# The second graph layer of a graph and expert kernel: 512 of 3125 destinations aggregated by row fetches instead of matrix products

## The chip, the cores and the metric

The kernel runs on one core of one Trainium2 chip. The time is the device time of one execution in microseconds (us). Times of single instructions come from one profiled execution. The engines are TensorE (PE; PEld is its weight load), VectorE (DVE), ScalarE (ACT), GpSimd (POOL) and SyncE (SP, which here only issues DMAs).

## The reference

A graph of 3125 nodes with 256 features and 103125 edges (sorted by destination, each node with a loop to itself) goes through four blocks, each added to its input: three graph attention layers, 16 experts of which each node uses two, one graph sum layer, and 8 experts of which each node uses one. The change concerns the second attention layer:

```python
def _gat_layer(x, src, dst, W, al, ar, b, n_nodes):
    h = x @ W
    el = h @ al
    er = h @ ar
    e = jax.nn.leaky_relu(el[src] + er[dst], NEG_SLOPE)
    m = jax.ops.segment_max(e, dst, num_segments=n_nodes)
    ex = jnp.exp(e - m[dst])
    s = jax.ops.segment_sum(ex, dst, num_segments=n_nodes)
    alpha = ex / s[dst]
    out = jax.ops.segment_sum(alpha[:, None] * h[src], dst, num_segments=n_nodes)
    return out + b
```

A destination has 33 edges on average.

## The kernel before, in words

Nodes lie in NT = 25 tiles of 128. `dense_attention` first builds a matrix of edge counts (uint8, sources on partitions, destinations along the row) and uses it in all three attention layers. The counts come from `Locator`, which reads the sorted edge lists with indirect DMAs (`find`, L1590) and sorts them into windows of five destinations (`finish`), and from `Counter`, which makes one-hot tiles on VectorE and ScalarE (L1662 to L1668), multiplies them on TensorE (L1683) and writes the counts with ScalarE (L1693). All this happens during the first layer.

The exponential of a leaky ReLU of el + er is factored: exp(0.2 el) is multiplied into the source row, and what is left per edge is max(exp(0.8 el), exp(-0.8 er)), up to a factor that cancels in the division. `Sources` holds this for one layer: `h` (25 tiles of 257 columns, the last one the factor itself, so that its sum is the divisor), `rho` = exp(0.8 el) and `lr`, the two products. `put` makes a tile of it: products (L1142), `lr` on VectorE (L1145), two exponentials and a scaled copy on ScalarE (L1146 to L1149).

A layer runs over 13 groups of destinations (`GROUPS`: 12 of 256, one of 53) and in each over the 25 source tiles s. One step is: VectorE makes a mask `pm` of 128 x 256 out of the destination terms `tau`, `rho` and the counts (L1310), and TensorE multiplies its two halves with the source row tile into two accumulators (L1313, in float32, two records per product). `pm` has six buffers. The last, small group makes six masks at a time (`few`, L1302, L1304) and uses half tiles (L1306). `terms` (L1250, L1253) makes `tau` for the next group at step 18, but for a layer's first group only when the layer begins. After a group, `divide` (at step 8 of the next group; L1339, L1340, L1348) divides by the sum and adds the bias, and `onward` (steps 10 and 13, one for each of the two tiles) transposes on TensorE (L1361), applies the ReLU on ScalarE (L1363) and calls `put` for the next layer's sources. In the third layer the result goes to a router instead.

While the first layer runs, `spare_rows` has GpSimd clear two tiles (L1320) and SP write them to the experts' row tables in DRAM in 34 transfers (L1727, up to 2.5 MB each). The order of instructions on each engine is set by a planner that uses its own estimates of durations and the order of issue; no order is written by hand.

Of the kernel before, what the change touches and what calls it, by code (L numbers as in the profile page):

```python
# [1 line left out]

# [7 lines left out]
F32 = mybir.dt.float32  # L10
# [712 lines left out]
def routed_experts(tc, x, room, ident, rows, sums, places, w1, w2, w3, load):  # L723
# [10 lines left out]
    with tc.tile_pool(name="rw", bufs=3) as ep, tc.tile_pool(name="rx", bufs=2) as xp, \  # L734
# [99 lines left out]
        def turn_more(slot, xs, s, own):  # L834
            ps = tp.tile([P, nh, P], F32, name="ps_x")
            for j in range(nh):
                nc.tensor.transpose(ps[:, j], s[:, j * P:(j + 1) * P], ident)
            hid = mp.tile([P, nh, P], F32, name="hid1")
            nc.scalar.copy(hid, ps)
            return slot, xs, hid, own  # L840
# [235 lines left out]
FINISH = [(0, 20), (2, 16), (4, 4), (5, 16)]  # L1076
TERMS = 18
EARLY = 8
SOME = 6
HELD = 64.0  # L1080

# [34 lines left out]
def block(big, d=D):  # L1116

    return big.tile([P, NT * (D + 1)], F32, name="big")[:, :NT * d].rearrange("p (t d) -> p t d", d=d)


class Sources:
# [3 lines left out]
    def __init__(self, tc, big, small):  # L1125
        self.nc = tc.nc
        self.h = block(big, D + 1)
        self.rho = small.tile([P, NT], F32, name="rho")
        self.lr = small.tile([P, 2, NT], F32, name="lr")

        for to in (self.h[:, NT - 1], self.rho[:, NT - 1:], self.lr[:, :, NT - 1]):
            self.nc.gpsimd.memset(to, 0.0)

    def put(self, pp, t, r, xTs, w, at=()):


        nc, n = self.nc, len(xTs)
        pss = []
        for i, xT in enumerate(xTs):
            ps = at[i] if i < len(at) else pp.tile([P, D + 2], F32, name="ps_m")  # L1140
            for k in range(KD):
                nc.tensor.matmul(ps[:r], xT[:, k], w[:, k], start=(k == 0), stop=(k == KD - 1))  # L1142
            pss.append(ps)
        for i, ps in enumerate(pss):
            nc.vector.tensor_scalar(self.lr[:r, :, t + i], ps[:r, D:], -HELD, HELD, op0=OP.max, op1=OP.min)  # L1145
        nc.scalar.activation(self.h[:r, t:t + n, D], self.lr[:r, 0, t:t + n], AF.Exp, scale=0.2)  # L1146
        nc.scalar.activation(self.rho[:r, t:t + n], self.lr[:r, 0, t:t + n], AF.Exp, scale=0.8)
        for i, ps in enumerate(pss):
            nc.scalar.activation(self.h[:r, t + i, :D], ps[:r, :D], AF.Copy, scale=self.h[:r, t + i, D:])  # L1149


def dense_attention(tc, dram, counts, x_in, big, ident, eps, layers, src, dst, rows, high, make_router, over):

# [9 lines left out]
    with tc.tile_pool(name="dw", bufs=1) as cp, tc.tile_pool(name="dwl", bufs=2) as wl, \  # L1163
         tc.tile_pool(name="dsm", bufs=2) as small:
        top = cp.tile([P, 3], F32, name="top")
        x = block(big)
        with tc.tile_pool(name="dp", bufs=6) as pmp, tc.tile_pool(name="ds", bufs=2) as sp, \
# [10 lines left out]
            kp = first.enter_context(tc.tile_pool(name="dpc", bufs=2, space=PSUM))  # L1178
            counter = Counter(tc, lp, ohp, locator, counts)
            pairs = [range(-(-c // (BATCH * WIN)), -(-(c + n) // (BATCH * WIN))) for c, n in GROUPS]  # L1180

# [63 lines left out]
            def terms(now, a):  # L1245
# [8 lines left out]
                return tau  # L1254

            third = ExitStack()
            later = []
            fills = []
            for i in range(3):
                last = i == 2  # L1260
                bt_i = bt
                if last:
                    wp = third.enter_context(tc.tile_pool(name="ro", bufs=2))
                    rp = third.enter_context(tc.tile_pool(name="ror", bufs=4))
                    zp = third.enter_context(tc.tile_pool(name="rop", bufs=1, space=PSUM))
                    router = make_router(third.enter_context(tc.tile_pool(name="roc", bufs=1)))
                    y_out = block(big)
                    nc.gpsimd.memset(y_out[:, NT - 1], 0.0)
                    nxt, we_n = None, None
                else:  # L1270
                    nxt = Sources(tc, big, small)
                    we_n, bt, products = attention_weights(tc, wl, cp, layers, i + 1, now.rho[:, NT - 1:])
                    products()
                for a, (c, n) in enumerate(GROUPS):
                    tiles = [(q, (c + q) // P, min(P, n - q)) for q in range(0, n, P)]

                    edges = counts_of(counts, a)
                    ahead = list(pairs[a + 1]) if i == 0 and a + 1 < len(GROUPS) else []
                    ready = []
                    tau = tau_next if a else terms(now, 0)  # L1280
                    acc = ap_.tile([P, 2, CHUNK], F32, name="acc")
# [7 lines left out]
                    for s in range(NT):  # L1289
                        if s == TERMS and a + 1 < len(GROUPS):  # L1290
                            tau_next = terms(now, a + 1)
                        if i == 0 and (a, s) in FINISH:
                            locator.finish(FINISH.index((a, s)) + 1, pp)
                        if i == 0 and (a, s) in FIND:
                            locator.find(FIND.index((a, s)) + 1, kp, tau[:, 0:1])
                        while later and later[0][0] == s:
                            later.pop(0)[1]()
                        if n <= P // 2:
                            if s % SOME == 0:
# [5 lines left out]
                            at = s % 2 * (P // 2)  # L1305
                            nc.tensor.matmul(acc[at:at + n, 0, :D + 1], few[:, s % SOME], now.h[:, s], start=(s < 2),  # L1306
                                             stop=(s >= NT - 2))
                        else:
                            pm = pmp.tile([P, PAIR], F32, name="pm")
                            nc.vector.scalar_tensor_tensor(pm[:, :n], tau[:, :n], now.rho[:, s:s + 1],  # L1310
                                                           edges[:, s, :n], op0=OP.max, op1=OP.mult)
                            for j, (q, t, r) in enumerate(tiles):
                                nc.tensor.matmul(acc[:r, j, :D + 1], pm[:, q:q + r], now.h[:, s], start=(s == 0),  # L1313
                                                 stop=(s == NT - 1))
                        while ready and ready[0][0] <= s:
                            counter.add(kp, ready.pop(0)[1])
                        if s == 2 and fills:

                            for e in empties:
                                nc.gpsimd.tensor_scalar(e, tau[:, 0:1], 0.0, None, op0=OP.mult)  # L1320
# [30 lines left out]

                    sooner = 2 if a == len(GROUPS) - 2 else 0
                    later.append((8 - sooner, divide))
# [3 lines left out]
                    for j, (q, t, r) in enumerate(tiles if not last else []):  # L1357
                        def onward(j=j, t=t, r=r, rest=rest, nxt=nxt, w=we_n):
                            ps = pp.tile([P, KD, P], F32, name="ps_m")
# [4 lines left out]
                            nxt.put(pp, t, r, [yT[:, :, :r]], w)  # L1364
                        later.append((10 + 3 * j, onward))
                    if i == 0 and a == 1:
                        fills, empties = spare_rows(tc, cp, *rows)
                if i == 0:
                    first.close()
                nc.vector.tensor_reduce(top[:, i:i + 1], now.lr, AX.XY, OP.max, apply_absolute_value=True)  # L1370
                now = nxt
            for _, what in later:
                what()
            router.finish(wp, zp, over)
            ps = pp.tile([3, P], F32, name="ps_m")
            nc.tensor.transpose(ps, top, ident)
            most = cp.tile([3, 1], F32, name="most")
            nc.vector.tensor_reduce(most, ps, AX.X, OP.max)
            ps = pp.tile([1, 3], F32, name="ps_m")
            nc.tensor.transpose(ps, most, ident[:3, :3])  # L1380
            nc.vector.tensor_reduce(high, ps, AX.X, OP.max)
# [137 lines left out]
class Locator:  # L1519
# [8 lines left out]
    def __init__(self, tc, cp, dram, src, dst, ident, room):  # L1528
# [36 lines left out]
        def find(j, pp, behind=None):  # L1565
# [8 lines left out]
            for q in range(NHEAD):  # L1574
                nc.tensor.matmul(ps[:PW], less[:rows, q, :PW], one[:rows], start=(q == 0), stop=(q == NHEAD - 1))
            at = cp.tile([P, 1], I32, name=f"at{j}")
            nc.vector.tensor_scalar(at[:PW], ps[:PW], -1.0, 0.0, op0=OP.add, op1=OP.max)
            if j < PARTS - 1:
                nc.vector.tensor_scalar(at[:PW], at[:PW], float(NR - RE // ER), None, op0=OP.min)
            for u, (of, name) in enumerate(self.lists):  # L1580
                if j == PARTS - 1:

                    to = dram.tile([E + RE], I32, name=name)
                    nc.sync.dma_start(to[:E].rearrange("(p e) -> p e", p=rows), of.rearrange("(p e) -> p e", p=rows))
                    none = cp.tile([1, RE], I32, name=name)
                    nc.gpsimd.memset(none, -WIN)
                    nc.sync.dma_start(to[None, E:], none)
                    of = to
                of = of.rearrange("(t e) -> t e", e=ER)
# [116 lines left out]


def spare_rows(tc, cp, rows0, rows1):

# [21 lines left out]
def routed(ctx: ExitStack, tc: tile.TileContext, i: dict, out: bass.AP, over):  # L1731
# [12 lines left out]
    with tc.tile_pool(name="counts", bufs=1) as kp:  # L1744
        counts = kp.tile([P, NT * ((len(GROUPS) - 1) * PAIR + 64)], U8, name="counts")
        x = dense_attention(tc, dram, counts, i["x"], big, ident, eps, layers, i["src"], i["dst"], (rows0, rows),
                            over[:, 3:4], lambda cp: Router(tc, cp, ident, eps, iota, count, rows0, sums,
                                                            i["L0_ffn_gate_w"], i["L0_ffn_gate_b"], more), over[:, 0:1])
        with tc.tile_pool(name="s0", bufs=1) as sp:
# [101 lines left out]
```

## Time and profile before

| | us |
|---|---|
| three runs, median (lowest to highest) | 1865.95 (1864.18 to 1867.11) |
| the profiled execution | 1866.04 |
| its span, first to last instruction | 1864.3 |
| first layer's steps begin | 72.0 |
| second layer's steps begin | 456.3 |
| third layer's steps begin | 755.5 |
| third layer ends, about | 1047 |

In the profile a group of instructions has its line in the kernel, engine and operation, then output <- inputs, shapes and a count, then busy time and the mean time of one in ns, and at last the idle time of that engine just before them with what ended it. In an order of time a line has start, length, engine, line, operation, names and how many instructions were merged into it. Matrix products overlap, so a single product's 382 ns is more than its share of the time: four of them follow each other in 0.87 us.

### The profile page before, as it was taken

Reading aid. Unit: us, or ns where it says so; the run is one execution under the profiler, and the core shown is the slowest. Engines: PE = TensorE matmul, PEld = TensorE weight load, DVE = VectorE, ACT = ScalarE, POOL = GpSimd, SP = SyncE. Lnnn points to the kernel's source line nnn. Section 1 sums busy time; section 2 is a strip of 40 time slices with the busy share of each in tenths; the row PEclk is TensorE's granted clock in tenths of the full one; section 3 lists DMA queues with packets and bytes.
Section 4 is the critical chain, followed back from the end, with each engine's and each line's share of the span. In section 5 each row is a group of like instructions: output and inputs, shape, how many; then the busy total and the mean of one; then the engine's idle time right before and its main releaser. Section 6 shows DMA issues by size and latency. Waiting matters only on the chain. (4 is left out here: it accounts for less than half of the span.)

```text
span 1864.3 us, 27270 instructions
## 1 busy us (share of the span) xinstructions
PE 1808.2 (97%) x9423; PEld 1427.1 (77%) x9423; DVE 971.2 (52%) x2644; ACT 717.5 (38%) x2052; POOL 309.6 (17%) x461
## 2 busy tenths in 40 slices
PE   6999999999999999999999799999989999999997
PEld 4788888887888888788888566666768886555886
DVE  5888888875555555677777622222252222224221
ACT  3766677671011111122222221211138998444221
POOL 4210100000000000133332322333300000222222
PEclk9999999999999999999999899999999999999999
DMA  3111113757000000111111286767430001733664
GB/s 116 33 36 46 48 62 129 312 213 306 1 1 1 1 1 7 41 46 46 46 46 42 76 261 188 213 180 200 91 80 1 1 1 35 245 128 143 219 211 129
DMA packets 105783, 185.42 MB, mean 99 GB/s; under 512 B 10968, under 2 KB 73849, under 8 KB 105600
## 3 DMA queue, kind: packets, MB, share of 16 engines
q1 hardware_dynamic: 74060, 127.06, 20.2%
q0 software_dynamic: 16432, 34.02, 6.9%
q10 hardware_dynamic: 15138, 22.44, 3.7%
q8 instruction: 79, 1.29, 0.3%
q14 instruction: 74, 0.61, 0.1%
HBM read 95.80 MB, written 89.77 MB: 100 GB/s over the span
## 5 line engine op out<-in xcount | busy, mean ns | idle before, releaser
L1313 PE MATMUL acc<-big,pm 128*128 128x257 f32 x3600 | 828.1, 382 | 3.1 <-DVE pm L1310 3.1
L1313 PEld LDWEIGHTS acc<-big,pm 128*128 128x128 f32 x3600 | 667.6, 190 | 94.6 <-DVE pm L1310 4.8
L1310 DVE SCALAR_TENSOR_TENSOR pm<-tau,rho,counts 128x256 f32<-128x256 f32 x900 | 427.5, 487 | 211.1 <-PE acc L1313 203.5
L774 PE MATMUL ps_h<-xsT,w 128*128 128x384 f32 x512 | 168.4, 487 | 0.6 <-ACT xsT L750 0.6
L1440 PE MATMUL acc<-msg,cr 128*128 128x512 f32 (+1 forms) x625 | 157.7, 403 | 0.1
L774 PEld LDWEIGHTS ps_h<-xsT,w 128*128 128x128 f32 x512 | 96.8, 190 | 66.9 <-issue 1.9
L1440 PEld LDWEIGHTS acc<-msg,cr 128*128 128x128 f32 (+1 forms) x625 | 114.7, 185 | 29.1 <-ACT cr L1436 1.2
L1436 ACT ACTIVATE cr<-counts 128x256 fp32r<-128x256 uint8 (+1 forms) x325 | 130.5, 402 | 14.4 <-PE acc L1440 6.9
L1693 ACT CAST counts<-acc_c 128x500 uint8<-128x500 f32 (+1 forms) x155 | 96.0, 678 | 93.9 <-PE acc_c L1683 93.8
L1023 PE MATMUL ps_y<-t_wd,hsT 128*128 x480 | 108.8, 380 | 0.4 <-ACT hsT L1051 0.4
L1668 DVE TENSOR_TENSOR ohk<-iota_k,key 128x2016 f16<-128x2016 f16 (+1 forms) x79 | 94.4, 1195 | 22.2 <-PE acc_c L1683 22.2
L777 ACT ACTIVATE silu<-ps_h 128x384 f32<-128x384 f32 x64 | 31.4, 491 | 182.1 <-PE ps_h L774 182.1
L1363 ACT ACTIVATE yT<-ps_m 128x256 f32<-128x256 f32 (+1 forms) x50 | 18.7, 375 | 214.4 <-PE ps_m L1361 214.4
L1023 PEld LDWEIGHTS ps_y<-t_wd,hsT 128*128 128x128 f32 x480 | 88.8, 190 | 11.6 <-ACT hsT L1051 0.6
L778 DVE TENSOR_TENSOR hid<-silu,ps_h 128x384 f32<-128x384 f32 x64 | 35.5, 554 | 114.4 <-PE ps_h L774 108.9
L1662 ACT ACTIVATE ohs<-iota_s,low 128x128 f16<-128x128 f16 x286 | 94.1, 401 | 0.0
L929 PE MATMUL ps_H<-big,t_w 128*128 128x512 f32 (+1 forms) x224 | 93.1, 552 | 0.7 <-ACT H L931 0.5
L794 POOL DMA_INDIRECT sums<-y,who x48 | 74.9, 1560 | 94.0 <-DVE y L792 70.3
L789 PE MATMUL ps_o<-w,hid 128*128 128x256 f32 x384 | 87.2, 379 | 0.0
L1683 PEld LDWEIGHTS <-ohs 128*128 128x128 f16 x1250 | 77.7, 98 | 10.9
L1683 PE MATMUL acc_c<-ohk,ohs 128*128 128x125 f16 x1250 | 84.5, 218 | 0.0
L789 PEld LDWEIGHTS ps_o<-w,hid 128*128 128x128 f32 x384 | 71.0, 190 | 8.8
(324 smaller groups left out, 1938.9 us busy)
## 6 DMA issues: line engine op xcount, KB each, us to landing
rows<-empty SPq DMA_DIRECT2D x16, 2564.0 KB, 18.6
w<-in_L_ffn_w_dram ACTq DMA_DIRECT2D x42, 512.0 KB, 4.9
hs<-rows SPq DMA_DIRECT2D x29, 641.0 KB, 4.3
big<-in_L_ffn_w_dram SPq DMA_DIRECT2D x30, 512.0 KB, 6.1
rows<-empty SPq DMA_DIRECT2D x16, 516.0 KB, 5.0
t_wd<-in_L_ffn_Wd_dram SPq DMA_DIRECT2D x8, 1024.0 KB, 11.9
xs<-rows SPq DMA_DIRECT2D x15, 387.0 KB, 3.4
bias<-in_L_ffn_bd_dram SPq DMA_DIRECT2D x30, 128.0 KB, 4.0
```

Source lines behind the costliest of these rows:

```text
L774: nc.tensor.matmul(ps, w[:, k, j * P:(j + 1) * P], xsT[:, k], start=(k == 0), stop=(k == KD - 1))
L789: nc.tensor.matmul(ps, hid[:, j, q * P:(q + 1) * P], o[:, j], start=(j == 0), stop=(j == nh - 1))
L929: nc.tensor.matmul(ps[:, :n], a[:, k, j * P:(j + 1) * P], xnT[:, k, c:c + n], start=(k == 0), stop=(k == KD - 1))
L1023: nc.tensor.matmul(ps, hsT[:, j], d[:, ds(e, 1), j, :].rearrange("p o f -> p (o f)"), start=(j == 0), stop=(j == nh - 1))
L1310: nc.vector.scalar_tensor_tensor(pm[:, :n], tau[:, :n], now.rho[:, s:s + 1], edges[:, s, :n], op0=OP.max, op1=OP.mult)
L1313: nc.tensor.matmul(acc[:r, j, :D + 1], pm[:, q:q + r], now.h[:, s], start=(s == 0), stop=(s == NT - 1))
L1436: nc.scalar.activation(cr[:, :n], edges[:, s, :n], AF.Copy, accum_out=seen[:, a * NT + s:a * NT + s + 1])
L1440: nc.tensor.matmul(acc[:r, j].rearrange("p h d -> p (h d)"), cr[:, q:q + r], msg[:, s].rearrange("p h d -> p (h d)"), start=(s == 0), stop ...
L1662: nc.scalar.activation(far[:, i], self.iota_s, AF.Abs, scale=-1.0, bias=self.low32[:, batch, i:i + 1])
L1668: nc.vector.tensor_tensor(to[:, i:tiles].rearrange("p t (x u) -> p t x u", u=2), iota.rearrange("p (x u) -> p x u", u=2)[:, None].to_broad ...
L1683: nc.tensor.matmul(acc[:, u], ohs[:, i], ohk[:, i, :KEYS], start=(t == 0), stop=(t == TW - 1))
L1693: nc.scalar.copy(to[:, :, d0 % PAIR:d0 % PAIR + whole * WIN].rearrange("p s (u d) -> p u s d", u=whole), acc[:, :whole])
```

## The change

In the second layer (i == 1) the loop over groups leaves out the first two (`APART` = 2, so `FEW` = 4 tiles, 512 destinations). For these a new class `Apart` follows the edges themselves:

- Each source tile of the second layer has `rho` in the same row as `h` (258 columns), and each tile, when made, is also written to a table in DRAM (`save`, 25 transfers by SP).
- During the first layer `bounds` and `rank` find, for each of the 512 destinations, where its edges begin and how many it has, and gather the edges' source numbers (`who`, five indirect DMAs). A destination has 38 places (`OWN`); what is over goes to a fifth tile of at most 128 destinations with 20 more places (`HEAVY`). These are 4 x 38 + 20 = 172 columns.
- In the second layer GpSimd fetches for each column one row per destination from the table (172 indirect DMAs of 128 rows of 258 words), in 45 batches of up to four, five batches ahead (`RING`). VectorE makes the coefficients of a batch and adds coefficient times row to an accumulator, one instruction per column. The fifth tile's sums are spread back to their destinations by one product on TensorE for each of the four tiles (`expand`).
- These pieces are placed between the steps of the remaining groups by a formula: column q at 19 + 1.31 q us, with 0.976 us per step. In this layer each engine keeps the order of issue (`manual_schedule`), and the way onward is cut in three pieces at steps +0, +1 and +4 with a copy of the raw product in between.
- The terms of the next layer's first group are made in the group before. The third layer's first group takes the source tiles from the fifth on, the first four last.
- One tile in the last expert block (`hid`) is now an earlier tile reused.

The core of the diff:

```diff
 class Sources:
-        self.h = block(big, D + 1)
-        self.rho = small.tile([P, NT], F32, name="rho")
+        self.h = block(big, ROW)
+        self.rho = self.h[:, :, D + 1]
...
+            def onward_steps(at, y, t, r, name, nxt, w, save):
...
+                return [(at, turn), (at + 1, multiply), (at + 4, keep)]
...
+                order = ExitStack()
+                if apart_now:
+                    order.enter_context(tc.manual_schedule())
                 for a, (c, n) in enumerate(GROUPS):
+                    if apart_now and a < APART:
+                        continue
...
-                    tau = tau_next if a else terms(now, 0)
+                    tau = tau_next or terms(now, a)
...
-                        if s == TERMS and a + 1 < len(GROUPS):
-                            tau_next = terms(now, a + 1)
+                        now_step[0] = (a - APART) * NT + s
+                        if s == (EARLIER if apart_now else TERMS):
+                            if a + 1 < len(GROUPS):
+                                tau_next = terms(now, a + 1)
+                            else:
+                                tau_next = None if last else terms(nxt, 0 if apart_now else APART)
...
+                            of = (s + FEW) % NT if last and a == 0 else s
...
+                        if apart_now and (a, s) == (APART, BEGIN):
+                            apart.begin(hp, hq, pp, now.lr)
+                        if apart_now and (a, s) == (APART, FETCH):
+                            for b in range(RING):
+                                apart.fetch(b)
+                        while soon and soon[0][0] <= now_step[0]:
+                            soon.pop(0)[1]()
+                        while now_apart and now_apart[0][0] <= now_step[0]:
+                            now_apart.pop(0)[1]()
...
+class Apart:
...
+    def save(self, sources, t, r):
+        self.nc.sync.dma_start(self.table[t * P:t * P + r], sources.h[:r, t])
...
+    def begin(self, hp, hq, pp, lr):
...
+        self.hots(hot)
...
+        for t in range(FEW):
+            nc.tensor.transpose(ps[:, t], hot[:, t], self.ident)
+        nc.scalar.copy(self.back, ps)
+        self.tau = hp.tile([P, FEW + 1], F32, name="apart_tau")
+        nc.scalar.activation(self.tau[:, :FEW], lr[:, 1, :FEW], AF.Exp, scale=-0.8)
+        ps = pp.tile([P, 1], F32, name="ps_m")
+        for t in range(FEW):
+            nc.tensor.matmul(ps, hot[:, t], self.tau[:, t:t + 1], start=(t == 0), stop=(t == FEW - 1))
+        nc.scalar.copy(self.tau[:, FEW:], ps)
...
+    def fetch(self, b):
...
+        for j in range(BATCHES_OF[b][2]):
+            nc.gpsimd.indirect_dma_start(
+                out=row[:, j], out_offset=None, in_=self.table[:, :],
+                in_offset=bass.IndirectOffsetOnAxis(ap=self.who[:, q + j:q + j + 1], axis=0))
...
+        def at(q):
+            time, whole = LANDED + EVERY * q, STEP * NT * (len(GROUPS) - 1 - APART)
+            return math.ceil(time / STEP if time < whole else whole / STEP + (time - whole) / LAST_STEP)
...
+            nc.vector.scalar_tensor_tensor(co[:, :m], row[:, :m, D + 1], self.tau[:, t:t + 1], self.real[:, q:q + m],
+                                           op0=OP.max, op1=OP.mult)
...
+                nc.vector.scalar_tensor_tensor(state["acc"], row[:, j, :D + 1], co[:, j:j + 1], state["acc"],
+                                               op0=OP.mult, op1=OP.add)
...
+            nc.tensor.matmul(ps, self.back[:, t], state["heavy"], start=True, stop=True)
```

## The prediction

> **What bounds the kernel now.** I read the summary of engines first, then the second graph layer alone as a stretch, TensorE's order of time through one of its groups, and last the rows of GpSimd and VectorE that can price the new work.
>
> ```profile
> PE 1808.2 (97%) x9423; PEld 1427.1 (77%) x9423; DVE 971.2 (52%) x2644; ACT 717.5 (38%) x2052; POOL 309.6 (17%) x461
> ```
>
> TensorE is busy for 97% of the span. The stretch of the second layer (first to last aggregation; columns: stretch, length, then PE, PEld, DVE, ACT, POOL busy, clock, DMA share, GB/s) says it more sharply:
>
> ```profile
> 456.30:755.50 299.20, 298.14 (x1426) 255.68 (x1426) 165.33 (x390) 32.42 (x115) 2.40 (x6) 1.00 0.01 4
> ```
>
> PE is busy 298.1 of 299.2 us, VectorE 165, GpSimd 2.4, the DMA engines 1%. So TensorE's work is this layer's length, and the units that the change loads are nearly idle. In order of time on PE, one group:
>
> ```profile
> 512.75 0.38 PE L1361 MATMUL ps_m<-ident,y 128*128 128x128 f32 x2
> 512.97 1.03 PE L1313 MATMUL acc<-big,pm 128*128 128x257 f32 x4
> 513.84 1.03 PE L1142 MATMUL ps_m<-we,yT 128*128 128x258 f32 x4
> ...
> 521.88 0.38 PE L1250 MATMUL ps_m<-ident,lr 128*128 128x128 f32 x2
> 522.09 14.92 PE L1313 MATMUL acc<-big,pm 128*128 128x257 f32 x68
> 536.85 0.38 PE L1361 MATMUL ps_m<-ident,y 128*128 128x128 f32 x2
> ...
> 755.47 8.95 PE L1313 MATMUL acc<-big,pm 128*128 128x257 f32 x40 [1.06 <-DVE pm L1310]
> ```
>
> A group of 256 destinations repeats every 536.85 - 512.75 = 24.10 us. One step (four records of L1313) takes 513.84 - 512.97 = 0.87 us, and 25 of them 21.7; the rest is two passes onward per group (transpose 0.22, product 0.87: 1.09 us each) and the 0.21 of the destination terms. The last line is the next layer's start: PE waits 1.06 us there for the first mask.
>
> The rows that price the change, first VectorE, then GpSimd:
>
> ```profile
> 455.75 3.26 DVE L1310 SCALAR_TENSOR_TENSOR pm<-tau,rho,counts 128x256 f32<-128x256 f32 x8 [1.69 <-ACT tau L1253]
> 447.96 0.49 DVE L1304 TENSOR_TENSOR few<-few,counts 128x318 f32<-128x318 f32 x1
> ```
> ```profile
> 125.28 1.28 POOL L1590 DMA_INDIRECT counts<-in_src_dram,at x1 [0.30 <-issue]
> ```
> ```profile
> L676 POOL DMA_INDIRECT rows<-row,g_to x50 | 50.5, 1009 | 41.1 <-DVE pm L1310 23.7 <-issue 10.7 <-DVE g_to L669 3.0
> L978 POOL DMA_INDIRECT rows<-row,to x25 | 24.5, 980 | 94.0 <-ACT row L974 72.0 <-ACT H L931 13.4 <-issue 4.3
> ```
>
> Eight masks run in 3.26 us: 0.41 us each when nothing holds them. An indirect DMA costs GpSimd 0.98 to 1.01 us as a scatter and 1.28 as a gather, and 0.30 us before the next one.
>
> [...] L676, issued in the third layer beside the masks, ranges from 0.972 to 1.085 us, L978 mostly stays at 0.975. [...] L676 lands 2.6 us after issue, the gathers of L1590 4.5.
>
> **The change part by part.** The layer's 12 full groups become 10. In program order of the changed kernel I count 50 masks and 100 aggregation products fewer, 172 row fetches on GpSimd, 172 sums and 45 coefficient operations on VectorE.
>
> *Removed on PE.* Two groups, 2 x 24.10 = 48.2 us.
>
> *Kept or added on PE.* Their four tiles still go onward: 4 x 1.09 = 4.4. Four spreading products of 257 columns, two records each: 4 x 0.43 = 1.7. At the first step four transposes and four one-column products, in order on PE: they wait for VectorE's four one-hot tiles, then for ScalarE's copy and exponential. Transposes 0.9, the copy of 512 columns about 0.6 (the same-sized copy hsT<-ps_cols has 0.589), exponential 0.2, products about 0.9, waits about 0.5: 3.1 us.
>
> *Starts of layers.* The terms of the next layer's first group are now made before it begins; the 1.06 us idle goes at both starts.
>
> *First layer.* Finding each destination's edges adds some 10 small products (1.2 us of PE), about 25 VectorE operations (some 10 us beside 305 busy in 375), five gathers and 25 saves of 128x258 rows. VectorE has slack and masks may run six steps ahead (six buffers, 5.2 us), which hides bursts of 3 to 4 us; I allow 1 us. Without that cover: 10 us. The saves share SP's queue with the 2.5 MB fills (L1727); only the last one matters, since the first fetch waits for it. In the trace the DMAs of the fills are done about 5 us into the layer, GpSimd's last clear at 461.4; the last save is issued at step 9 (9 x 0.964 + 3.1 = 12 us in) and lands in about 2.4 (row y<-in_x, same size), so the first fetch starts about 15 us into the layer. The first sum stands at step 25, about 27 us. Four fetches and a landing, 15 + 4 x 1.31 + 4.5 = 25, arrive before it.
>
> *GpSimd's fetches.* The code sets one sum per 1.31 us of an assumed step of 0.976; at the real 24.10/25 = 0.964 that is 1.294 us per sum. Fetches take duration + 0.30. Bounds: 0.975 + 0.30 = 1.28 (scatter) and 1.33 + 0.30 = 1.63 (median of the gathers of L1590). I take 1.31, as L676: it has the same 128 rows of 258 words and runs beside masks, whereas L1590 takes 125 rows and runs beside the f16 compares. Then GpSimd is busy 172 x 1.31 = 225 of 260 us and a deficit of 172 x 0.016 = 2.7 us meets a lead of about 2. Each fetch is refilled some 20 sums ahead, so landing is hidden. A fetch moves 132 KB; L676's DMAs, the same size, ran at this rhythm.
>
> *VectorE.* Per sum of 1.294 us: masks 1.34 x 0.41 = 0.55; the sum 0.41 to 0.53 (L1304, which needs the result before it, starts 0.53 after that), middle 0.45; coefficient 0.05; the rest, of the divisions and small columns, 0.08. Together 1.13, 87%: close, but below PE. VectorE runs in order, so a late row holds the masks queued behind that sum, and PE waits for these.
>
> *ScalarE* gains a 0.4 us copy per tile (the raw products), in a layer where it is 11% busy: nothing. Order of issue replaces a planner's order; in both, the product stands one step (0.87 us) behind its transpose, and the ReLU between takes 0.38. I allow 2 us for collisions with the passes of the four tiles and late rows.
>
> *Other edits.* The strides of 258, the in-place hid and the rotated sources of the third layer's first group: no time by themselves; the rotation lets the four tiles come last.
>
> **Sum.** Second layer after: 10 x 24.10 = 241.0, the small group 755.47 - 745.05 - 1.06 = 9.4, onward 4.4, spreading 1.7, first step 3.1, collisions 2.0: 261.6, against 755.47 - 456.29 = 299.2: minus 37.6. First layer: + 1.2 + 1.0 - 1.06 = + 1.1. Together - 36.5. The profiled execution took 1866.04 (span 1864.3 and 1.7 around it), 0.1 above the median 1865.95 of the runs; so 1866.0 - 36.5 = 1829.5.
>
> **Rivals.** *Rows later than planned, part of the gain lost (1838 to 1862).* If a fetch costs 1.45 us [...], the last row lands at 15 + 172 x 1.45 + 3 = 267.4, and the 9 us of the small group come after it: 276.8, 15 more, 1845. A sum that costs 0.7 instead of 0.45 makes VectorE the bound at about 1.38 per sum and gives 172 x 0.09 = 15 too. For it: the 0.972 to 1.085 spread. Against: the spread is a tenth only, with VectorE 75% busy there (194 of 260 us, 770 to 1030).
>
> *Slower: the gather's own price.* If direction, not the 125 rows or the f16 compares, makes L1590 dear, then 1.63 holds: 15 + 172 x 1.63 + 4.5 + 9.4 = 309, 10 more than now; with the first layer's 1.1, 1877. It is slower from about 1.57 us per fetch. For it: the only gathers in the trace cost that, to 1.28 at the least. Against: L676's rows are those of the fetches, L1590's 125 partitions are not. That VectorE is 87 to 89% busy beside L1590 (stretches 72 to 130 and 130 to 200) cuts both ways: it may be why they are slow, and VectorE will be as busy after, if with f32 sums in place of f16 compares.
>
> *No effect* from another cause, such as a stage after the third layer that takes the gain back: the experts' stage starts from the end of that layer, and no view shows it waiting for a clock of its own, so little speaks for it: 1866.
>
> **How the numbers follow.** A difference of 0.2% (3.7 us) is about what a measurement can tell from none. Forecast (1822 to 1838) 0.65; late rows, partial gain 0.20; slower 0.08; no change 0.03; more gain, under 1822, if first step, collisions and bursts cost nothing (7 us) 0.04. Faster: 0.65 + 0.20 + 0.04 = 0.89. Leaving out the last case, no change, slower and the upper quarter of the partial one (0.05), together 0.20, gives 1822 to 1850.
>
> **What would show it.** In the profile after: the second layer 262 us long with PE above 97% busy; fetches 1.0 us long and 1.3 apart; GpSimd 85% and VectorE near 87% busy there; sums of 0.4 to 0.5; no large wait of a coefficient operation for a DMA; about 3 us of PE's time at the first step; the starts of both layers without the 1.06. Wrong if fetches come over 1.4 us apart, PE waits tens of us for masks behind sums, or the first layer grows by over 5 us.

## The result and the profile after

| | before | changed |
|---|---|---|
| median (lowest to highest), us | 1865.86 (1864.18 to 1867.11), 4 runs | 1839.81 (1835.95 to 1840.10), 4 runs |
| the profiled execution, us | 1866.04 | 1840.01 |
| steps of the first layer begin | 72.0 | 67.8 |
| first layer's steps | 384.3 | 385.7 |
| second layer's steps | 299.2 | 273.35 |
| third layer's steps, to its small group | 285.4 | 285.3 |
| from there to the end of the execution | 825.2 | 827.8 |

The ratio is 0.9856 [0.9839, 0.9873]: 26 us faster where 36.5 were forecast. In the profiled runs the parts add up to -4.2 + 1.4 - 25.8 - 0.1 + 2.6 = -26.1, so nearly the whole difference is the second layer. A later run of the same kernel at another place was slower than the kernel before; that is told below, and it limits all of this.

The changed kernel's page, engines over the span:

```profile
PE 1771.2 (96%) x9249; PEld 1389.5 (76%) x9249; DVE 1017.4 (55%) x2865; ACT 725.4 (39%) x2078; POOL 501.5 (27%) x636
```

Its second layer as one stretch (columns as in the prediction):

```profile
453.54:726.89 273.35, 262.36 (x1242) 218.89 (x1241) 209.60 (x573) 40.28 (x141) 190.66 (x187) 1.00 0.33 89
```

TensorE's work fell as forecast, but 273.35 - 262.36 = 11.0 us of idle time came in, where 1.1 had been. The layer's waits (who <- for whom: us, times, longest) name the way:

```profile
DVE apart_co L1950 <- DMA apart_row<-apart_rows,apart_who: 28.3, 24, 3.1
PE acc L1391 <- DVE pm L1388: 7.7, 10, 2.1
PE ps_m L1289 <- DVE apart_acc L1336: 1.4, 1, 1.4
PE acc L1383 <- DVE few L1381: 1.0, 1, 1.0
PE ps_m L1919 <- ACT apart_tau L1916: 0.8, 1, 0.8
```

VectorE waits 24 times for fetched rows (`apart_co` is the coefficients of a batch, the first to read its rows), 28.3 us in all, and TensorE waits 7.7 us for the masks that stand behind. One such place in order of time, all engines but ScalarE and the weight loads:

```profile
526.05 1.29 POOL L1933 DMA_INDIRECT apart_row<-apart_rows,apart_who  x1 [0.30 <-DVE apart_acc L1959]
527.64 0.95 POOL L1933 DMA_INDIRECT apart_row<-apart_rows,apart_who  x1 [0.30 <-issue]
528.76 0.22 DVE L1950 SCALAR_TENSOR_TENSOR apart_co<-apart_row,apart_tau,apart_real 128x4 f32<-128x4 f32 x1 [2.26 <-DMA apart_row<-apart_rows,apart_who]
...
529.42 0.48 DVE L1388 SCALAR_TENSOR_TENSOR pm<-tau,big,counts 128x256 f32<-128x256 f32 x1
...
529.96 1.35 PE L1391 MATMUL acc<-big,pm 128*128 128x257 f32 x5 [1.10 <-DVE pm L1388]
```

The coefficients of a batch wait 2.26 us for its last row, the mask behind them starts at 529.42, and TensorE, whose stock of six masks has run out, has stood for 1.10. The groups of the fetches, the sums and the coefficients:

```profile
L1933 POOL DMA_INDIRECT apart_row<-apart_rows,apart_who x172 | 186.7, 1085 | 62.6 <-issue 39.3 <-DMA apart_rows<-big 10.5 <-DVE pm L1388 4.6
L1959 DVE SCALAR_TENSOR_TENSOR apart_acc<-apart_row,apart_co,apart_acc 128x257 f32<-128x257 f32 x167 | 80.9, 485 | 1.6
L1950 DVE SCALAR_TENSOR_TENSOR apart_co<-apart_row,apart_tau,apart_real 128x4 f32<-128x4 f32 x41 | 9.1, 222 | 28.7 <-DMA apart_row<-apart_rows,apart_who 28.3
```

A fetch takes 1.085 us on average. The first starts at 470.4, the last at 708.2: (708.2 - 470.4) / 171 = 1.39 us apart, with never more than the usual 0.30 between them. GpSimd is thus occupied without a break, and too slow for sums that are due every 1.294 us.

### The profile page after: what moved, and what is told of

Same layout as the page of the kernel before. It is cut to its first block, busy times and chain, and to the rows that moved or that the text cites. A ratio compares the mean times of both kernels' runs of the same rounds, so it can differ in the third digit from the quotient of the medians.

```text
span 1838.2 us, 27323 instructions
## 1 busy us (share of the span) xinstructions
PE 1771.2 (96%) x9249; PEld 1389.5 (76%) x9249; DVE 1017.4 (55%) x2865; ACT 725.4 (39%) x2078; POOL 501.5 (27%) x636
## 5 line engine op out<-in xcount | busy, mean ns | idle before, releaser
L1391 PE MATMUL acc<-big,pm 128*128 128x257 f32 x3400 | 787.7, 383 | 8.9 <-DVE pm L1388 8.9
L1391 PEld LDWEIGHTS acc<-big,pm 128*128 128x128 f32 x3400 | 628.6, 190 | 99.4 <-DVE pm L1388 15.4
L1388 DVE SCALAR_TENSOR_TENSOR pm<-tau,big,counts 128x256 f32<-128x256 f32 x850 | 398.3, 487 | 99.9 <-PE acc L1391 96.0
L1933 POOL DMA_INDIRECT apart_row<-apart_rows,apart_who x172 | 186.7, 1085 | 62.6 <-issue 39.3
L1959 DVE SCALAR_TENSOR_TENSOR apart_acc<-apart_row,apart_co,apart_acc 128x257 f32<-128x257 f32 x167 | 80.9, 485 | 1.6
```

The lines of the kernel that those rows point to most:

```text
L1933: nc.gpsimd.indirect_dma_start(out=row[:, j], out_offset=None, in_=self.table[:, :], in_offset=bass.IndirectOffsetOnAxis(ap=self.who[:, q ...
```

## The experiments

The kernels ran in three sets, each set on one chip beside runs of the kernel before: here "place B" for the first four kernels, "place C" for the next four, "place D" for the last four, and "place A" for the result. Each place was used at one time only, and for A the chip is not known, so chip and time of the run are not told apart. Before took 1863.5, 1864.4 and 1865.5 us at B, C and D. The theories: **A**, VectorE's operations with two inputs in SBUF hold GpSimd's fetches up, rows come late, and masks queue behind sums; **B**, the fetches are slow by themselves or by their transfers; **C**, VectorE's load or order is the limit and the fetches are not.

| kernel | place | median (lowest to highest), us | ratio to before there | second layer, us | fetch, mean ns |
|---|---|---|---|---|---|
| no_sums | B | 2112.75 (2108.38 to 2117.30) | 1.1337 [1.1304, 1.1370] | 314.0 | 985 |
| one_fetch | B | 2070.85 (2064.90 to 2073.45) | 1.1094 [1.1063, 1.1125] | 276.5 | 1004 (20 of them) |
| psum_sums | B | 1887.89 (1880.39 to 1893.42) | 1.0110 [1.0070, 1.0150] | 320.8 | 988 |
| psum_both | B | 1905.40 (1900.44 to 1910.35) | 1.0226 [1.0197, 1.0255] | 334.6 | 956 |
| fewer | C | 1835.82 (1835.10 to 1838.01) | 0.9846 [0.9829, 0.9862] | 268.2 | 1074 |
| later | C | 1829.51 (1827.05 to 1831.22) | 0.9811 [0.9792, 0.9830] | 260.4 | 1066 |
| planner | C | 1883.92 (1883.01 to 1886.05) | 1.0105 [1.0088, 1.0122] | 314.9 | 1028 |
| early_terms | C | 1863.17 (1859.92 to 1866.15) | 0.9989 [0.9982, 0.9997] | 298.6 | none |
| after_again | D | 1893.72 (1888.98 to 1898.75) | 1.0150 [1.0121, 1.0179] | 325.9 | 1026 |
| psum_again | D | 1884.27 (1877.58 to 1896.47) | 1.0126 [1.0083, 1.0170] | 311.9 | 987 |
| psum_both_again | D | 1906.79 (1905.94 to 1908.42) | 1.0228 [1.0211, 1.0245] | 339.8 | 957 |
| later_fewer | D | 1885.26 (1877.98 to 1886.89) | 1.0101 [1.0074, 1.0128] | 316.5 | 1031 |

The second layer is measured from its first mask product to that of the third (in later and later_fewer, where two products of the third layer come 1.2 us early, to the product behind the last of the second). no_sums leaves out all sums but a destination's first; one_fetch leaves out the fetches after the first twenty, so that the sums read rows fetched earlier. In both, what follows the third layer becomes about 230 us longer, probably because tokens are routed otherwise; only the second layer is read there.

### The sums left out (no_sums)

```diff
-            else:
-                nc.vector.scalar_tensor_tensor(state["acc"], row[:, j, :D + 1], co[:, j:j + 1], state["acc"],
-                                               op0=OP.mult, op1=OP.add)
```

> Leaves out 167 of the 172 sums (each tile keeps only its first row, so the second layer's output for 512 destinations is not the reference's); all fetches, coefficients and passes onward stay. In the changed kernel the 172 fetches take 1.387 us each from start to start (238.6 us), though most of them are 0.96 us long. Theory A (VectorE's operations with two inputs in SBUF hold GpSimd up [...]): with VectorE's load down from 77% to about 48%, fewer fetches are stretched, about 1.32 each, and the second layer goes from 273.4 us to about 264, the whole to about 1830. Theory B (the stretch comes from the DMA side or from GpSimd itself): 1.387 stays, the layer stays within 2 us of 273. Theory C (fetches are not the limit, VectorE's load is): 1.387 stays and the layer drops to about 262.

The layer took 314 us, longer than with the sums, which no theory had. Its waits hold gaps of TensorE of up to 5.2 us that end with "issue", the profile's word for no cause that it shows. The fetches did become shorter, 985 ns.

### Twenty fetches only (one_fetch)

```diff
+        if b >= RING:
+            self.ring[b] = self.rows_at[b % RING]
+            return
...
+        self.rows_at[b] = row
```

> Only the first 20 row fetches are made and their rows are used over and over (so the output for 512 destinations is not the reference's); sums, coefficients, order of issue and passes onward stay. If late rows are what the second layer lost against the forecast (A or B), no operation of VectorE waits for a row and the layer takes about 261 to 263 us in place of 273.4, the whole about 1829. If the order of issue or VectorE's load is the cause (C), the layer stays at 271 to 274.

276.5 us, though no row could be late: 260.5 to the small group, 16 from there. Two parts of the first stretch, while the twenty fetches ran and after them:

```profile
476.00:505.00 29.00, 22.91 (x87) 17.88 (x86) 13.72 (x37) 0.88 (x3) 17.94 (x18) 0.80 0.35 87
505.00:716.80 211.80, 211.80 (x1000) 184.02 (x999) 173.78 (x478) 32.05 (x112) 1.48 (x2) 0.99 0.01 2
```

Beside the fetches TensorE is idle for 6.1 us and its granted clock falls to 0.80 on average, which no theory named; the runs at D show that this was the place. From 505 on it is busy for the whole 211.8 us, with the sums in their old places and VectorE 82% busy. So where rows are there, neither VectorE's load nor the order of issue costs time in these groups, against C. The small group is another matter. TensorE waits there 0.85 us for a mask and 1.45 for the last tile's sums, as in the changed kernel (1.0 and 1.4 above), and here no row was late: the last sums and the last tile's way onward fall together. (Its granted clock is also 0.50 for 3.4 us here.)

### The sums in PSUM (psum_sums), and the masks' terms too (psum_both)

```diff
-                state["acc"] = self.hp.tile([P, D + 1], F32, name="apart_acc", bufs=2)
+                state["acc"] = self.hq.tile([P, D + 1], F32, name="apart_acc")
...
```
```diff
+                if taus and a > APART:
+                    tau = taus[0][:, a % 2]
+                else:
+                    tau = sp.tile([P, PAIR], F32, name="tau")
...
+                    taus.append(hq.tile([P, 2, PAIR], F32, name="tau_ps"))
...
```

> The sums' accumulator lies in PSUM instead of SBUF, so each of the 167 sums reads only one operand from SBUF. Same arithmetic. Theory A: only the masks (0.41 us of each 0.96) can then hold GpSimd up; the fetches come about 1.32 us apart, the layer takes about 264 to 268 us and the whole 1831 to 1835. Theory B: 1.387 and 273 stay. If PSUM operands are slower on VectorE (sums over 0.55 us), the layer gets longer under every theory.

> As the run before, and the destination terms of the second layer's masks lie in PSUM too: hardly any VectorE operation of that layer reads two operands from SBUF. Theory A: the fetches are all about 0.96 us long and 1.26 apart (172 x 1.26 = 217 us), no row is late, the layer takes about 261 to 263 us, the whole 1827 to 1830. Theory B: 1.387 and 273 stay.

A few copies by ScalarE, from PSUM back to SBUF, go with both. The fetches shortened as A said, 1085 to 988 to 956 ns, and yet the layers grew to 321 and 335 us. The two findings contradict each other under every theory; the runs at place D show what else stood in these traces.

### Fewer slots (fewer) and a slower rhythm (later)

```diff
-OWN = 38
-HEAVY = 20
+OWN = 37
+HEAVY = 17
```
```diff
-EVERY = 1.31
+EVERY = 1.39
...
+                soon.clear()
```

> 37 places per destination instead of 38 and 17 instead of 20 for those over it: 165 fetches and sums instead of 172; no edge is lost with these inputs. If the fetches are the second layer's clock (A, B), the layer gets shorter by about 7 x 1.39 = 9.7 us, until TensorE's own work of about 260 bounds it: 264, the whole about 1830. If they are not (C), it gains at most 7 x 0.45 = 3 us of VectorE's time.

> The sums are placed in VectorE's order at 1.39 us each instead of 1.31, the rhythm that the fetches had; nothing else changes (the list of passes is emptied after the layer). If late rows hold up the masks queued behind them, TensorE idles less while the groups run, but the last row still lands at the same time, about 262 us into the layer, with one tile's way onward after it: the layer takes 266 to 272 us. If the end of the fetches alone counts, 271 to 274. If late rows are not the cause, the later sums lengthen it: 276 or more.

At place C nothing stood in the way, and later is the test of the whole layer. VectorE has the same 172 sums and 45 coefficient operations, only each due when its row is there:

```profile
455.39:715.79 260.40, 258.57 (x1238) 219.20 (x1238) 201.97 (x557) 38.72 (x136) 185.88 (x177) 1.00 0.34 94
```
```profile
L1934 POOL DMA_INDIRECT apart_row<-apart_rows,apart_who x172 | 183.3, 1066 | 62.6 <-issue 43.6 <-DMA apart_rows<-big 10.5 <-DVE pm L1388 4.9
L1951 DVE SCALAR_TENSOR_TENSOR apart_co<-apart_row,apart_tau,apart_real 128x4 f32<-128x4 f32 x41 | 9.0, 220 | 2.2 <-DMA apart_row<-apart_rows,apart_who 2.2
```

VectorE's waits for rows fell from 28.3 to 2.2 us, TensorE's idle time from 11.0 to 1.8, the layer from 273.35 to 260.40, although the fetches are hardly faster (1066 ns). Of these 13 us, 9.9 lie before the small group (258.73 against 248.86): there sums had been promised rows that were not there, with masks behind them. Together with one_fetch that settles C against in the groups, and the chain "rows late, masks behind sums, TensorE waits" for. The other 3.1 us lie in the small group (14.6 against 11.5) and come from the place of the last sums: seven of them and the last tile's way onward now run on into the third layer, which is 0.7 us longer. That is also why the layer came out under the 266 to 272 expected, which had put that way onward at its end. Both layers together gain 12.3 us. With fewer slots and the old rhythm the rows stay late (23.1 us of waits) and only 5 us are gained, 2 of them before the small group and 3 in it; the layer expected was 264.

### The order left to the planner (planner), and the early terms alone (early_terms)

```diff
-                if apart_now:
-                    order.enter_context(tc.manual_schedule())
```

> The same kernel without the hand-kept order of issue in the second layer: the planner places sums, masks and fetches by its own estimates. If the order of issue costs TensorE time (C), the layer gets shorter than 273 by some us. If it protects the masks from sums that wait for rows, it gets longer: the planner may put sums ahead of masks whose rows are not there; 280 to 300.

314.9 us, above the 280 to 300 expected, and 19.5 us slower in all than before. The waits of its layer:

```profile
DVE apart_co L1948 <- DMA apart_row<-apart_rows,apart_who: 61.8, 22, 5.9
PE acc L1389 <- DVE pm L1386: 24.0, 12, 3.8
PE ps_m L1161 <- ACT yT L1291: 15.0, 4, 9.1
```

The same instructions in an order that puts masks behind rows that come later: 61.8 us of waits instead of 28.3, and TensorE stands 39 us for masks and passes onward. The order of issue is worth 42 us in this layer (314.9 against 273.35), more than the whole gain.

For early_terms, the kernel before makes the terms of a layer's first group in the layer before it and has no other edit:

```diff
-                        if s == TERMS and a + 1 < len(GROUPS):
-                            tau_next = terms(now, a + 1)
+                        if s == TERMS:
+                            tau_next = terms(now, a + 1) if a + 1 < len(GROUPS) else None if last else terms(nxt, 0)
...
```

> The kernel before with one part of the change alone: the terms of the next layer's first group are made in the group before, so that the first mask does not wait. Expected: the idle 1.06 us of TensorE at the starts of the second and the third layer go, each layer's start moves up by about 1 us, the whole by about 2 us (0.1%), which is near what the times can tell.

0.9989 [0.9982, 0.9997], or 0.6 to 3.4 us, in keeping with two waits of 1.06; in the traces the first two layers are together 1.4 us shorter. The third layer's start there:

```profile
751.43 0.43 PE L1250 MATMUL ps_m<-ident,lr 128*128 128x128 f32 x2
...
753.66 8.95 PE L1313 MATMUL acc<-big,pm 128*128 128x257 f32 x40
```

The products of the terms stand before the layer, and no wait is noted at its first mask.

### The changed kernel once more, beside three others

> The changed kernel once more, unaltered, beside the two that follow it. In the earlier runs with the sums in PSUM, without the sums and with few fetches, TensorE gave its semaphore updates 1.4 to 5 us apart instead of 0.87 while the fetches ran, and its granted clock then fell to 0.5 for 3 to 20 us at a time; in the changed kernel, run at another time, it did not. If those stalls belong to the edits: 1840, second layer 273, granted clock 1.00 throughout it. If they belong to the place or time of the run: the changed kernel shows them too wherever the two kernels beside it do, and all three show them or none does.

> The kernel with the running sums of the fetched rows in PSUM once more, unaltered. If the stalls of TensorE belong to the edit: 1888 again, clock at 0.5 from about 30 us after the layer's first fetch. If they do not and VectorE's operations with two inputs in SBUF are what holds the fetches up (theory A): no stall, fetches of 1.00 us mean instead of 1.085, a period of 1.30, VectorE's waits for rows under 5 us instead of 28, the second layer some 262 us and the kernel 1828 to 1832. If the stretch comes from the transfers or GpSimd alone (theory B): fetches stay at 1.08, rows 25 to 28 us late in all, 1838 to 1842.

> The kernel with the sums and the broadcast terms of the masks in PSUM once more, unaltered. Theory A without stalls: fetches at 0.96 us throughout, period 1.26, no row late, second layer 261 to 263, kernel 1827 to 1833. Theory B: fetches at 1.08, as the changed kernel. If the stalls belong to the edit: 1905 again.

> Two edits together: sums due 1.39 us apart instead of 1.31, and 165 slots instead of 172. The rhythm alone gave 1829.5, the slots alone 1835.8. With the rhythm right no row is late any more, so if lateness of rows was all that the slots took away, the two together give what the rhythm alone gives, 1829 (1827 to 1831). If the sums also take room on VectorE that masks need, or set the end of the groups, 7 sums fewer give 3 to 9 us more: 1821 to 1826.

after_again is the changed kernel, with no edit. It took 1893.7 us: 28 us slower than before, 54 slower than itself at place A. later_fewer is later and fewer together, and psum_again and psum_both_again are the kernels of place B; all four were slower than before, and so the stall belongs to the place or its time and not to the edits. The second layer of after_again, and two parts of it:

```profile
457.31:783.22 325.91, 277.83 (x1243) 226.54 (x1242) 209.10 (x573) 40.25 (x141) 180.72 (x187) 0.93 0.28 75
476.00:491.00 15.00, 15.00 (x71) 12.89 (x70) 8.70 (x23) 0.38 (x1) 11.65 (x12) 1.00 0.43 105
491.00:518.00 27.00, 9.69 (x25) 6.38 (x24) 6.58 (x17) 0.76 (x2) 14.48 (x16) 0.62 0.30 79
```

TensorE is idle for 48 us, and the granted clock, 1.00 in this layer at place A, is 0.93 on average and 0.62 in the second part. In order of time on TensorE:

```profile
476.44 15.05 PE L1391 MATMUL acc<-big,pm 128*128 128x257 f32 x68
493.24 1.13 PE L1391 MATMUL acc<-big,pm 128*128 128x257 f32 x4 [1.74 <-issue]
497.46 2.03 PE L1391 MATMUL acc<-big,pm 128*128 128x257 f32 x4 [3.09 <-DVE pm L1388]
499.29 0.63 PE L1289 MATMUL ps_m<-ident,y 128*128 128x128 f32 x2
500.31 2.08 PE L1391 MATMUL acc<-big,pm 128*128 128x257 f32 x4 [0.40 <-DVE pm L1388]
514.48 2.06 PE L1161 MATMUL ps_m<-we,yT 128*128 128x258 f32 x4 [12.08 <-issue]
```

The fetches began at 474.14. TensorE first works off what it has (68 records in a row), then gets one mask every few us, then stands for 12. On VectorE one of the masks of that time, and on ScalarE and GpSimd the end of the gap:

```profile
492.70 0.48 DVE L1388 SCALAR_TENSOR_TENSOR pm<-tau,big,counts 128x256 f32<-128x256 f32 x1 [0.81 <-PE acc L1391]
...
509.09 0.96 POOL L1933 DMA_INDIRECT apart_row<-apart_rows,apart_who  x1 [0.30 <-issue]
...
514.00 0.38 ACT L1291 ACTIVATE yT<-ps_m 128x256 f32<-128x256 f32 x1 [36.97 <-remote]
```

VectorE waits for TensorE to give a mask buffer back, and ScalarE waits until 514.00 for a transpose that TensorE's own record has long done (499.29). What is late is not rows but TensorE's word that it is done. The trace also records the updates of the semaphores; counted from it, those of the DMAs (nearly all of them the fetches') beside the small writes (4 bytes, 16 to a fetch), which they match in number at place A:

| stretch, us | | TensorE's updates | DMA updates recorded | small writes |
|---|---|---|---|---|
| 470 to 500 | changed, place A | 38 | 322 | 336 |
| | after_again, place D | 21 | 73 | 294 |
| 500 to 720 | changed, place A | 242 | 2462 | 2448 |
| | after_again, place D | 179 | 582 | 2171 |

At place A TensorE's updates come 0.87 us apart, one per step. In after_again they come 1.4 to 2.2 us apart from some 8 us after the first fetch, while the matrix products' records still follow each other without a gap, and then up to 7.7. Then several come at once, three to seven of them 0.06 us apart, too close for work (a step takes 0.87): updates held back and let go. Counted as three or more less than 0.1 us apart, the second layers of the eight traces at B and D have 56 such bursts. Every one lies in a pause of the fetches of at least 1.9 us or after the last of them, 0.9 to 3.9 us after a fetch ended, and none while fetches follow each other. In the second layers of the changed kernel at A and of fewer, later and planner at C there is none. one_fetch shows that the fetches do it: its one burst, of seven, comes 2.5 us after the twentieth fetch ended, and from 505 on the updates are again 0.87 us apart in the median, as at A and C.

So at B and D TensorE's updates are held back while fetched rows arrive; VectorE and ScalarE wait for them, TensorE runs dry, and then its granted clock is cut as well. The cuts in the traces are to 0.50, for 3.4, 6.8, 13.7, 17.1 or 20.5 us. In the 3.4 us before a cut TensorE stood for 1.7 to 3.4 us in after_again and for 2.0 to 3.4 in planner; a gap of 2.06 us in the changed kernel (at 692.5) had no cut behind it. TensorE's records look busy meanwhile (68 in a row for 15.05 us above), but the ends of products are modelled in the profile, so they don't tell when a product was done.

**What stays open.** Why two of four places do this, and whether it is the chip or the time of the run. The transfers themselves are about as fast there: a packet of fetched rows takes a median 174 ns at D and 167 at A. From 500 to 720 us the DMA updates recorded in after_again are a quarter of the small writes (582 of 2171), and no run here shows why. Since every time here comes from a recorded execution, none tells whether the recording takes part. Which property of the fetches does it, bytes or the number of packets, was not tried.

**What place D says of theory A.** The fetches can be compared inside one place, and even inside one run. At D, under the same stall, their mean falls 1026, 987, 957 ns as first the sums and then the masks lose one of their two inputs in SBUF, in the groups of psum_again and psum_both_again:

```profile
L1933 POOL DMA_INDIRECT apart_row<-apart_rows,apart_who x172 | 169.7, 987 | 104.7 <-issue 44.9 <-DVE apart_acc L1959 35.3 <-DMA apart_rows<-big 10.5
```
```profile
L1940 POOL DMA_INDIRECT apart_row<-apart_rows,apart_who x172 | 164.5, 957 | 135.2 <-DVE apart_acc L1966 73.6 <-issue 43.0 <-DMA apart_rows<-big 10.5
```

Stalled TensorE leaves VectorE idle, which alone would shorten fetches, so I sorted them by what stood beside each. Fetches with 0.6 us or more of VectorE's masks, sums and coefficients beside them took 1.116 us in the changed kernel at A (some 125 of 172), 1.07 in after_again, 1.007 in psum_again and 0.957 in psum_both_again (some 100 each). Those with none beside them (7 in the changed kernel) took 0.956 in all four, the longest 0.96. So it is the two SBUF inputs: the same operations beside the same fetches cost nothing once one input lies in PSUM. B falls as the cause of the long fetches.

## Why the forecast was right in sign and 10 us short

**The rhythm of the fetches is the step that was mis-sized.** The prediction took 1.31 us, from a scatter that runs beside masks. It was 1.39: 0.956 + 0.30 = 1.26 undisturbed, and 0.13 for VectorE's two-input operations. Against sums due each 1.294 us that is 172 x 0.096 = 16.5 us of deficit instead of 2.7. It shows as 28.3 us of VectorE's waits, of which TensorE's six masks of stock hide a good part. The allowance of 2.0 us for "collisions" was to hold late rows too; 273.35 - 261.6 = 11.7 more came. later shows that most of this is the rows: with them in time the groups are 9.9 us shorter, and the rest lies in the small group, in waits for the last sums that only this allowance covered. That the median of later is the forecast's 1829.5 to the digit is chance: the kernel before took 1864.4 there, so it gains 34.9 us. The prediction had the spread of L676 beside masks, 0.972 to 1.085 us, and read it as the size of the effect; the traffic of sums on top of masks gives a mean of 1.085, and 0.956 with one input of each in PSUM. So what happened is the first rival, rows later than planned, at about half its price (1.39 instead of 1.45), and the result lies at the low edge of its 1838 to 1862.

**What held.** Two groups, kept passes, spreading, first step and collisions: with the rows in time, in later, the second and third layers (to its small group) together take 546.4 us, where the forecast gives 261.6 + 285.4 = 547.0. The first step, in order on TensorE of the changed kernel:

```profile
453.54 1.13 PE L1391 MATMUL acc<-big,pm 128*128 128x257 f32 x4
454.51 0.60 PE L1913 MATMUL ps_m<-ident,apart_row 128*128 128x128 f32 x4
455.89 1.05 PE L1919 MATMUL ps_m<-apart_tau,apart_row 128*128 128x1 f32 x8 [0.78 <-ACT apart_tau L1916]
456.81 1.98 PE L1391 MATMUL acc<-big,pm 128*128 128x257 f32 x8
459.42 2.00 PE L1391 MATMUL acc<-big,pm 128*128 128x257 f32 x8 [0.64 <-DVE pm L1388]
```

456.81 - 454.51 = 2.3, and 0.64 for a mask behind it: 2.9 for 3.1. The first line also answers for the starts of layers, no wait is noted at it. The first layer grew by 1.4 us (forecast 1.1), a sum takes 0.485 us and 0.40 from start to start (0.45), the third layer is unchanged. The gather's own price, the slower rival, was wrong: 0.956, not 1.33. Whether the 125 rows or the f16 compares had made those gathers dear, no run here shows. VectorE was 79% busy while the fetches ran (187.8 of 238.6 us), not near 87%, as the sums came more slowly. The first fetch starts 16.8 us into the layer (15).

**What was missed besides.** The steps begin 4.2 us sooner. This is luck and not the change's doing: after_again, the same kernel, begins at 71.9. In all traces the start goes with the granted clock before it: 71.2 to 72.1 where the clock falls to 0.50 for 6.8 us in that stretch, as in before, 69.8 to 69.9 where it does for 3.4, and 67.8 to 67.9 where it doesn't, as in the changed kernel. After the third layer 2.6 us came back, so that 1.6 us of the gain in the profiled pair lie outside the layers.

**What the forecast had no place for.** It took TensorE's work as the layer's length and the fetches' transfers of 132 KB, one per 1.31 us, as free, since a third-layer scatter of that size ran so. At places B and D that step fails: while fetches run there, TensorE's updates come late. The kernel is then slower than before by 1.5% [1.2, 1.8], outside the range that was given, and by none of the mechanisms of the rivals. later_fewer at D loses as well (1.0101), so the better rhythm doesn't mend it. The result above is one side of this.

The version to keep, where updates are not held back, is later: 1829.5 us, 0.9811 [0.9792, 0.9830]. Which side a run is on has to be measured.

## What to carry to other kernels

A coefficient operation that waited 2.26 us for its row held the mask behind it on VectorE, and TensorE stood for 1.10: place an instruction that waits for a transfer by the rhythm that the producer reaches under load, not by the one it has alone; 6% of rhythm was worth some 10 us here. When a change loads an idle unit, price it beside the work that it will meet (a fetch cost 0.96 us alone and 1.12 beside two-input operations in SBUF). And run the final version at more than one place and time before the gain is believed.

## What had not been expected of the hardware

- At two of four places, at D with the very program of A, TensorE's semaphore updates came 1.4 to 7.7 us apart instead of 0.87 while row fetches of 128 x 258 words ran, 1.26 to 1.4 us apart; one layer took 325.9 us against 273.35.
- In the four runs compared a fetch took 0.956 us to within 0.01 where no mask, sum or coefficient operation of VectorE stood beside it, and single fetches reached 2.48 us in the changed kernel, where such operations with two SBUF inputs did.
- After some gaps of TensorE its granted clock was 0.50 for at least 3.4 us: in planner seven times in the second layer without any held updates, once after a single gap of 2.06 us. After a gap as long in the changed kernel it stayed at 1.00.
